# A second LayerNorm whose half sums are put together on GpSimd, a piece at a time

## The chip, the core and the metric

The kernel runs on one core of a Trainium2 chip. The metric is device time in microseconds of one launch. The engines that matter here are VectorE (DVE in the profile), GpSimd (POOL), ScalarE (ACT), TensorE (PE) and SyncE (SP, which issues DMAs). Each engine takes the instructions of its own queue strictly in order, and engines wait for one another through semaphores.

## What is computed

The reference is one layer in two halves on `x` of shape (4, 1024, 256). The first half is a Mamba block (gated selective scan) with a residual and a LayerNorm; the second is a mixture of experts (one shared expert and the best two of eight) with a residual and a second LayerNorm:

```
def _layernorm(x, axis=-1, eps=1e-05):
    m = jnp.mean(x, axis=axis, keepdims=True)
    v = jnp.var(x, axis=axis, keepdims=True)
    return (x - m) / jnp.sqrt(v + eps)
...
    x = _layernorm(x + _L0_attn_ref(x, ...), axis=-1)
    x = _layernorm(x + _L0_ffn_ref(x, ...), axis=-1)
    return x
```

The change is in the second of these two LayerNorms: for each of 4096 tokens, the mean and variance of 256 numbers, and then (x - m) / sqrt(v + 1e-5).

## The kernel before

**The long part.** The 4096 tokens are cut into 8 chunks of 512 (`CHUNKS`). For each chunk and each of 16 states the loop over `order` runs a scan (`scan`, `outputs`). Beside it, generators are advanced a step at a time: `front` (projections and convolution of the next chunk), `tail` (output projection, first LayerNorm, router and the lists of rows by expert of the chunk before) and `moe` (the experts' matrix products, block by block). Experts' results are added by DMA into a buffer in device memory, `sums_of`, which already holds the first LayerNorm's output.

**The end.** After all experts there is a conditional block for blocks left over (no instruction crosses it), and then `finish()` (L1003 on). It is the only caller of the second LayerNorm. It cuts the 32 tiles of 128 tokens into five pieces of 4, 8, 8, 8 and 4 tiles, and issues at once, on SyncE, the five loads of the pieces from `sums_of` into SBUF tiles `o_0` to `o_4` (L1011). Then, for each piece in turn:

1. `stats` (L215 to L220, called in the loop over `pieces`, L1038): for each tile of 128 tokens a VectorE `bn_stats` (L219) writes six numbers a token: count, mean, and sum of squared deviations, for each of two halves of the row; a VectorE `bn_aggr` (L220) puts the halves together into mean and variance, `mv`.
2. A VectorE instruction adds 1e-5 to the variances of the piece (`var`, L1043).
3. `rsqrt` (L204 to L212): a first guess by integer arithmetic, and three Newton steps of four instructions each, 13 instructions in all, each of which needs the one before. Its tiles are [128, tiles of the piece]. It runs on GpSimd for the first four pieces and on VectorE for the last (`newton`).
4. On the same engine, `shift` = -(mean x rstd), two instructions (L1047, L1048).
5. `scale` of the piece **before** this one: 5 of 8 tiles (3 of 4) on ScalarE (L1023), the rest on VectorE (L1029), and two stores, one on ScalarE's queue (L1034) and one on SyncE's (L1035). The last piece is scaled after the loop.

The buffers of `small` are double: `mv2`, `var2`, `root`, `nt` and `shift` each have two, so piece i+2 takes the buffer of piece i, and can write it only when its last reader is done. The last readers of `root` and `shift` are the `scale` instructions.

**Order.** The framework lays out each engine's queue before the run, with the program's order as priority, but an instruction that it holds to be ready may be put ahead of one that it holds to be waiting. The order is then fixed, and so are the waits. Only what is marked `keep_in_program_order` (the VectorE part of `scale`) is bound.

The lines outside `finish` that the diff touches are in `tail` and `by_expert`, once a chunk: `probs` (L626, router), `row` (L688), `mine` (L652 and L692) and `ee` (L749).

Of the kernel before, what the change touches and what calls it, by code (L numbers as in the profile page):

```python
# [8 lines left out]
F32 = mybir.dt.float32  # L9
AF = mybir.ActivationFunctionType  # L10
ALU = mybir.AluOpType
AX = mybir.AxisListType

P = 128
NSEQ, SEQ, D = 4, 1024, 256
# [5 lines left out]
E = 8  # L21
# [49 lines left out]
def mamba_moe_kernel(  # L71
# [18 lines left out]
    nc = tc.nc  # L90

    const = ctx.enter_context(tc.tile_pool(name="const", bufs=1))
    small = ctx.enter_context(tc.tile_pool(name="small", bufs=2))
    one = ctx.enter_context(tc.tile_pool(name="one", bufs=1))
# [105 lines left out]
    def rsqrt(v, name, engine=nc.gpsimd):  # L200

        shape = list(v.shape)
        y = small.tile(shape, F32, tag="root", name=f"root_{name}")
        engine.tensor_scalar(  # L204
            y.bitcast(I32), v.bitcast(I32), -0.5, float(0x5F3759DF), ALU.mult, ALU.add
        )
        t = small.tile(shape, F32, tag="nt", name=f"nt_{name}")
        for _ in range(3):
            engine.tensor_tensor(t, y, y, ALU.mult)  # L209
            engine.tensor_tensor(t, t, v, ALU.mult)  # L210
            engine.tensor_scalar(t, t, -0.5, 1.5, ALU.mult, ALU.add)  # L211
            engine.tensor_tensor(y, y, t, ALU.mult)  # L212
        return y

    def stats(src, mv, tiles, name):  # L215

        for t in range(tiles.start, tiles.stop):
            st = small.tile([P, 6], F32, tag="bnst", name=f"bnst_{name}_{t}")
            nc.vector.bn_stats(st, src[:, t, :])  # L219
            nc.vector.bn_aggr(mv[:, t, :], st)  # L220
# [320 lines left out]
    def tail(b, c):  # L541
        s = f"{b}_{c}"
# [13 lines left out]
        mv = small.tile([P, TT, 2], F32, tag="mv", name=f"mv_{s}")  # L556
        for half in range(2):
            po = ps_mix.tile([P, TT // 2, D], F32, tag="mix", name=f"po_{s}_{half}")
            for i in range(TT // 2):
                t = half * TT // 2 + i  # L560
# [17 lines left out]
        var = small.tile([P, 2, TT], F32, tag="var", name=f"var_{s}")  # L578
# [3 lines left out]
        rstd = rsqrt(var, f"l1_{s}")  # L582
# [18 lines left out]
        few = [P, TT, E]  # L601
# [21 lines left out]
        scaled(summed, rstd[:, 0, :], mv[:, :, 0], summed, f"l1_{s}")  # L623
        nc.scalar.dma_start(own_sums.rearrange("(t p) d -> p t d", p=P), summed)
        yield
        probs = small.tile(few, F32, tag="probs", name=f"probs_{s}")  # L626
        nc.scalar.activation(probs, logits, AF.Sigmoid)
        nc.scalar.activation(probs2, logits, AF.Sigmoid)
        full = [P, TT, E, E]
# [1 line left out]
        own = probs.unsqueeze(3).to_broadcast(full)  # L631
# [20 lines left out]
        mine = one.tile([P, TOPK, TT, E], F32, tag="mine", name=f"mine_w_{s}")  # L652
# [19 lines left out]
        nc.scalar.copy(combT, pc)  # L672
        channels[b, c] = (x1T, combT)
        yield from by_expert(b, c, hn, rank, weights, both, sofar, part, flat)

    def by_expert(b, c, hn, rank, weights, both, sofar, part, flat):

        s = f"{b}_{c}"
# [3 lines left out]
        few = [P, TT, E]  # L682
# [2 lines left out]
        nc.tensor.matmul(place[:, 0:TT, :], lhsT=upper, rhs=both, start=False, stop=True)  # L685
        yield from wait(1, 2)
        counts = place[:, TT, :]
        row = one.tile(few, F32, tag="row", name=f"row_{s}")  # L688
        nc.vector.tensor_tensor(
            row, place[:, 0:TT, :], starts.unsqueeze(1).to_broadcast(few), ALU.add  # L690
        )
        mine = one.tile([P, TOPK, TT, E], F32, tag="mine", name=f"mine_{s}")  # L692
# [53 lines left out]
        nc.vector.tensor_reduce(so_far, over, AX.X, ALU.add)  # L746
        nc.vector.tensor_tensor(there, so_far, done, ALU.subtract)
        nc.vector.tensor_tensor(left, so_far, done, ALU.subtract)
        ee = one.tile([P, E, E], F32, tag="ee", name=f"ee_{s}")  # L749
        nc.vector.tensor_tensor(ee, before, left.unsqueeze(1).to_broadcast([P, E, E]), ALU.mult)  # L750
        scatter(0)
        yield from wait(1, 2)
# [250 lines left out]
    def finish():  # L1003


        tags = ["xs", "delta", "y"]
        pieces, at = [], 0
        for i, tiles in enumerate((4, 8, 8, 8, 4)):
            o = two.tile([P, tiles, D], F32, tag=tags[i % 3], name=f"o_{i}")
            rows = slice(at * P, (at + tiles) * P)  # L1010
            nc.sync.dma_start(  # L1011
                o, sums_of[P + rows.start : P + rows.stop, :].rearrange("(t p) d -> p t d", p=P)
            )
            dst = out.rearrange("b s d -> (b s) d")[rows, :].rearrange("(t p) d -> p t d", p=P)
            pieces.append((o, dst))
            at += tiles

        def scale(o, dst, rstd, shift):
            tiles = o.shape[1]
            on_act = (5 * tiles + 4) // 8  # L1020
            for t in range(tiles):
                if t < on_act:
                    nc.scalar.activation(  # L1023
                        o[:, t, :], o[:, t, :], AF.Identity,
                        bias=shift[:, t : t + 1], scale=rstd[:, t : t + 1],
                    )
                else:
                    tc.keep_in_program_order(
                        nc.vector.tensor_scalar(  # L1029
                            o[:, t, :], o[:, t, :], rstd[:, t : t + 1], shift[:, t : t + 1],  # L1030
                            ALU.mult, ALU.add,
                        )
                    )
            nc.scalar.dma_start(dst[:, 0:on_act, :], o[:, 0:on_act, :])  # L1034
            nc.sync.dma_start(dst[:, on_act:, :], o[:, on_act:, :])  # L1035

        ahead = None
        for i, (o, dst) in enumerate(pieces):  # L1038
            tiles = o.shape[1]
            mv = small.tile([P, tiles, 2], F32, tag="mv2", name=f"mv2_{i}")  # L1040
            stats(o, mv, slice(0, tiles), f"l2_{i}")
            var = small.tile([P, tiles], F32, tag="var2", name=f"var2_{i}")
            nc.vector.tensor_scalar(var, mv[:, :, 1], 1e-5, None, ALU.add)  # L1043
            newton = nc.gpsimd if i + 1 < len(pieces) else nc.vector
            rstd = rsqrt(var, f"l2_{i}", newton)
            shift = small.tile([P, tiles], F32, tag="shift", name=f"shift_l2_{i}")
            newton.tensor_tensor(shift, mv[:, :, 0], rstd, ALU.mult)  # L1047
            newton.tensor_scalar(shift, shift, -1.0, 0.0, ALU.mult, ALU.add)  # L1048
            if ahead is not None:
                scale(*ahead)  # L1050
            ahead = o, dst, rstd, shift
        scale(*ahead)


# [33 lines left out]
    for i, step in enumerate(order):  # L1088
# [3 lines left out]
        for k in range(KB):  # L1092
# [15 lines left out]
            if k == KB // 2 - 1:  # L1108
                if late is not None:
                    outputs(*late)  # L1110
                    if n == 0:
                        list_of = ending if place + 1 == len(chunks) else beside
                        list_of.append(tail(*chunks[place - 1]))
                if n == 0 and place + 1 < len(chunks):
                    beside.append(front(*chunks[place + 1]))
                if n == 3:
                    beside.append(scans[b, c][4]())
                if n == N // 2 and place + 2 < len(chunks):
                    xs_in[chunks[place + 2]] = load_x(*chunks[place + 2])
                side(beside)  # L1120
# [9 lines left out]
    keep(*late[0:2])  # L1130
    outputs(*late)
    ending.append(tail(*chunks[-1]))
    while ending:
        side(ending)
# [5 lines left out]
    with tc.If(left > 0):  # L1140
        first, last = last, last + len(at_end)
        units += at_end
        for u in range(first, last):
# [5 lines left out]
            while pending:  # L1149
                pending.pop(0)()  # L1150
    finish()


# [52 lines left out]
```

## Time and profile before

| what | value |
|---|---|
| time, median of 3 runs (lowest, highest) | 1592.58 us (1586.84, 1595.74) |
| the profiled execution, its own time | 1591.91 us |
| its span, first to last instruction | 1590.2 us |
| loads of the five pieces issued (L1011) | from 1556.16 us |
| first `bn_stats` of piece 0; of piece 1 | 1560.00 us; 1563.29 us |
| ScalarE starts scaling pieces 0, 1, 2, 3 | 1566.30, 1571.64, 1576.20, 1580.81 us |
| last store issued | 1584.96 us |
| `bn_stats` (L219), `bn_aggr` (L220) in the end stage | 32 of 410 ns, 32 of 178 ns (median) |
| small GpSimd instructions of the stage | 60, about 200 ns each |

All times of instructions are counted from the start of the span. The stage in question is its last 34 us, 2% of it. A line of the timeline has the start, the time from the start of its first to the end of its last instruction, the engine, the line of the code, the operation, out<-in with shapes, the number of instructions, and in brackets how long the engine had been idle and who released it. Consecutive instructions of one engine can overlap in these records: a start may lie before the end of the one before.

### The profile page before, as it was taken

The page shows a single profiled execution, that of the slowest core. Times are in us where ns is not written, and L with a number is a line of the kernel's source. Part 1 is how long each engine was busy: PE and PEld are TensorE (multiplying, and loading weights), DVE is VectorE, ACT ScalarE, POOL GpSimd, SP SyncE. Part 2 cuts the span into 40 slices and gives each one's busy share as a digit, 9 for nine tenths or more (in the row PEclk, how much of TensorE's full clock was granted, in tenths as well). Part 3 has the DMA queues.
Part 4 walks back from the last instruction along what each step waited for, and adds up shares of the span by engine and source line. Part 5 has one row for each costly group of instructions (what it writes and reads, how often), then busy time and mean ns, then how long its engine had stood idle before and what let it go on. Part 6 is the DMA issues. An engine that isn't in the chain of part 4 may idle for free. (4 is left out here: it accounts for less than half of the span.)

```text
span 1590.2 us, 20804 instructions
## 1 busy us (share of the span) xinstructions
PE 1254.7 (79%) x6639; PEld 970.3 (61%) x6639; DVE 1279.8 (80%) x1422; ACT 1065.6 (67%) x2345; POOL 1141.6 (72%) x886
## 2 busy tenths in 40 slices
PE   5588467865688788879798889888879889899990
PEld 2356324652356666677567756776667768789990
DVE  3999899989997898999998999899989899320005
ACT  5757458764778578877788778766886666434442
POOL 2468975798578876998789978997699887431223
PEclk8699678987788999999999999899899999999995
DMA  4000000440016562475236633563166538659996
GB/s 121 1 0 1 26 14 17 146 119 17 13 61 192 173 182 64 147 220 168 50 124 204 190 80 122 159 197 107 35 209 185 153 116 249 177 153 323 315 273 217
DMA packets 160275, 211.64 MB, mean 133 GB/s; under 512 B 20617, under 2 KB 138130, under 8 KB 160162
## 3 DMA queue, kind: packets, MB, share of 16 engines
q1 hardware_dynamic: 135954, 181.75, 35.2%
q0 software_dynamic: 17216, 21.57, 7.6%
q10 hardware_dynamic: 6992, 6.95, 1.3%
q8 instruction: 54, 0.88, 0.2%
q14 instruction: 59, 0.48, 0.1%
HBM read 178.97 MB, written 31.27 MB: 132 GB/s over the span
## 5 line engine op out<-in xcount | busy, mean ns | idle before, releaser
L530 POOL TENSOR_TENSOR y<-y,hs 128x2048 f32<-128x2048 f32 x128 | 597.1, 4665 | 81.2 <-DVE hs L529 80.8
L513 ACT ACTIVATE da<-delta,chan_sb 128x512 f32<-128x512 f32 x512 | 353.0, 697 | 193.1 <-DVE hs L516 190.6
L929 PE MATMUL pd<-w,h 128*128 128x256 f32 x1600 | 386.7, 386 | 22.5 <-ACT h L909 11.5
L929 PEld LDWEIGHTS pd<-w,h 128*128 128x128 f32 x1600 | 298.8, 193 | 92.8 <-issue 20.5
L516 DVE TENSOR_TENSOR_SCAN hs<-da,state,hs 128x512 f32<-128x512 f32 x256 | 317.8, 1270 | 27.1 <-ACT da L513 26.0
L900 PEld LDWEIGHTS pu<-xT,w 128*128 128x128 f32 x2176 | 276.6, 204 | 64.7 <-ACT xT L883 45.5
L900 PE MATMUL pu<-xT,w 128*128 128x128 f32 x2176 | 281.3, 288 | 28.0 <-ACT xT L883 28.0
L529 DVE TENSOR_TENSOR hs<-hs,pb 128x2048 f32<-128x2048 f32 x128 | 290.7, 2271 | 3.3 <-PE pb L430 1.6
L909 ACT ACTIVATE h<-pu,wb 128x128 f32<-128x128 f32 x800 | 229.3, 368 | 71.9 <-PE pu L900 67.2
L516 DVE TENSOR_TENSOR_SCAN hs<-da,hs 128x512 f32<-128x512 f32 x204 | 240.9, 1209 | 21.2 <-ACT da L513 20.7
L449 POOL TENSOR_TENSOR hs<-xs,b 128x512 f32<-128x512 f32 x118 | 170.6, 1448 | 67.9 <-ACT b L442 48.9
L444 DVE TENSOR_TENSOR hs<-xs,pb 128x1536 f32<-128x1536 f32 (+1 forms) x115 | 197.9, 1722 | 13.2 <-ACT b L442 7.5
L962 POOL DMA_INDIRECT sums<-rb,xb x68 | 108.0, 1588 | 131.3 <-ACT xT L883 43.8
L293 PE MATMUL pi<-hT,w_in_sb 128*128 128x512 f32 x256 | 143.0, 683 | 32.6 <-DVE xs L325 12.3
L430 PE MATMUL pb<-parts,pick 128*128 128x512 bf16 x243 | 98.2, 407 | 77.1 <-DVE hs L529 27.6
L900 PEld LDWEIGHTS pu<-x1T,w 128*128 128x128 f32 x1024 | 130.9, 203 | 13.8 <-issue 10.0
L900 PE MATMUL pu<-x1T,w 128*128 128x128 f32 x1024 | 136.4, 290 | 0.0
L219 DVE BATCH_NORM_STATS2 bnst_l<-o 128x6 f32<-128x256 f32 x32 | 11.9, 411 | 153.9 <-DMA o<-sums 153.9
L293 PEld LDWEIGHTS pi<-hT,w_in_sb 128*128 128x128 f32 x256 | 49.9, 213 | 97.3 <-issue 34.2
L562 PE MATMUL po<-w_out_sb,y 128*128 128x256 f32 x256 | 70.0, 435 | 36.6 <-POOL y L552 29.1
L562 PEld LDWEIGHTS po<-w_out_sb,y 128*128 128x128 f32 x256 | 55.5, 222 | 56.3 <-POOL y L552 36.3
L705 POOL DMA_INDIRECT rows<-hn,to x64 | 63.4, 990 | 32.1 <-issue 15.8
(198 smaller groups left out, 1555.8 us busy)
## 6 DMA issues: line engine op xcount, KB each, us to landing
w<-in_ew SPq DMA_DIRECT2D x136, 1024.0 KB, 5.7
w<-in_sw SPq DMA_DIRECT2D x16, 1024.0 KB, 5.3
xb<-rows SPq DMA_DIRECT2D x68, 129.0 KB, 5.1
x<-in_x SPq DMA_DIRECT2D x8, 512.0 KB, 4.2
sums<-summed ACTq DMA_DIRECT2D x8, 512.0 KB, 3.0
sums<-rs POOLq DMA_DIRECT2D x16, 256.0 KB, 6.6
o<-sums SPq DMA_DIRECT2D x3, 1024.0 KB, 8.8
out<-o ACTq DMA_DIRECT2D x3, 640.0 KB, 3.3
```

The costliest lines, as they stand in the source:

```text
L293: nc.tensor.matmul(pi, lhsT=w_in_sb[:, k, m * P : (m + 1) * P], rhs=hT[:, k, :], start=(k == 0), stop=(k == KD - 1),)
L444: nc.vector.tensor_tensor(hs[:, 0:on_pool, :], xs[:, 0:on_pool, :], pb.unsqueeze(1).to_broadcast([P, on_pool, TC]), ALU.mult,)
L449: nc.gpsimd.tensor_tensor(hs[:, k, :], xs[:, k, :], copy, ALU.mult)
L513: nc.scalar.activation(da, delta[:, k, :], AF.Exp, scale=chan_sb[:, k, CA + n : CA + n + 1])
L516: nc.vector.tensor_tensor_scan(hs[:, k, :], da, scaled_inputs.pop(0) if by_pe(step) else hs[:, k, :], 0.0 if c == 0 else state[:, k, n : n ...
L529: nc.vector.tensor_tensor(hs, hs, pb.unsqueeze(1).to_broadcast([P, KB, LEN[b, c]]), ALU.mult)
L530: nc.gpsimd.tensor_tensor(y, y, hs, ALU.add)
L562: ins = nc.tensor.matmul(po[:, i, :], lhsT=y[:, k, t * P : (t + 1) * P], rhs=w_out_sb[:, k, :], start=(k == 0), stop=(k == KB - 1),)
L900: nc.tensor.matmul(pu[:, i, :], lhsT=w[:, k, at : at + P], rhs=xT[:, k, :], start=(k == 0), stop=(k == KD - 1),)
L909: nc.scalar.activation(t[:, i, :], pu[:, i, :], AF.Relu, bias=wb[:, m : m + 1])
L929: nc.tensor.matmul(pd, lhsT=hidden[h][:, i, :], rhs=w[:, m, :], start=(m == 0), stop=(m == HB - 1 and e is None),)
L962: nc.gpsimd.indirect_dma_start(sums_of[:, :], bass.IndirectOffsetOnAxis(xb[:, TOKEN : TOKEN + 1].bitcast(U32), 0), rb, None, compute_op=AL ...
```

## The change

The loop over the pieces calls one of two functions. The last piece takes `own`: what was done before, all on VectorE. The first four take `by_halves`: VectorE runs only the `bn_stats`, into one tile `halves` of [128, tiles, 6]; the `bn_aggr` of each tile and the VectorE instruction for `var` are gone. GpSimd then makes variance and mean of all the tiles of the piece with strided operands: six instructions for `var` (difference of the two means, its square, a quarter of it plus 1e-5; sum of the two sums of squares, divided by 256; the sum of both), the same `rsqrt`, and three for `shift` (sum of the means, times `rstd`, times -0.5) where there were two. That is 22 GpSimd instructions a piece in place of 15. To make room in SBUF, three small tiles of the long part share buffers: `probs` has one buffer in place of two, `row` lies in the tag `o` (used otherwise in the set-up only), and `ee` in the tag `mine`.

```diff
-        probs = small.tile(few, F32, tag="probs", name=f"probs_{s}")
+        probs = small.tile(few, F32, tag="probs", name=f"probs_{s}", bufs=1)
...
-        row = one.tile(few, F32, tag="row", name=f"row_{s}")
+        row = one.tile(few, F32, tag="o", name=f"row_{s}")
...
-        ee = one.tile([P, E, E], F32, tag="ee", name=f"ee_{s}")
+        ee = one.tile([P, E, E], F32, tag="mine", name=f"ee_{s}")
...
+        def own(i, o):
+            tiles = o.shape[1]
+            mv = small.tile([P, tiles, 2], F32, tag="mv2", name=f"mv2_{i}")
+            stats(o, mv, slice(0, tiles), f"l2_{i}")
+            var = small.tile([P, tiles], F32, tag="var2", name=f"var2_{i}")
+            nc.vector.tensor_scalar(var, mv[:, :, 1], 1e-5, None, ALU.add)
+            rstd = rsqrt(var, f"l2_{i}", nc.vector)
+            shift = small.tile([P, tiles], F32, tag="shift", name=f"shift_l2_{i}")
+            nc.vector.tensor_tensor(shift, mv[:, :, 0], rstd, ALU.mult)
+            nc.vector.tensor_scalar(shift, shift, -1.0, 0.0, ALU.mult, ALU.add)
+            return rstd, shift
+
+        def by_halves(i, o):
+            tiles = o.shape[1]
+            st = small.tile([P, tiles, 6], F32, tag="halves", name=f"halves_{i}")
+            for t in range(tiles):
+                nc.vector.bn_stats(st[:, t, :], o[:, t, :])
+            var = small.tile([P, tiles], F32, tag="var2", name=f"var2_{i}")
+            apart = small.tile([P, tiles], F32, tag="nt", name=f"apart_{i}")
+            shift = small.tile([P, tiles], F32, tag="shift", name=f"shift_l2_{i}")
+            g = nc.gpsimd
+            g.tensor_tensor(apart, st[:, :, 1], st[:, :, 4], ALU.subtract)
+            g.tensor_tensor(apart, apart, apart, ALU.mult)
+            g.tensor_scalar(apart, apart, 0.25, 1e-5, ALU.mult, ALU.add)
+            g.tensor_tensor(var, st[:, :, 2], st[:, :, 5], ALU.add)
+            g.tensor_scalar(var, var, 1.0 / D, 0.0, ALU.mult, ALU.add)
+            g.tensor_tensor(var, var, apart, ALU.add)
+            rstd = rsqrt(var, f"l2_{i}", g)
+            g.tensor_tensor(shift, st[:, :, 1], st[:, :, 4], ALU.add)
+            g.tensor_tensor(shift, shift, rstd, ALU.mult)
+            g.tensor_scalar(shift, shift, -0.5, 0.0, ALU.mult, ALU.add)
+            return rstd, shift
+
         def scale(o, dst, rstd, shift):
...
         for i, (o, dst) in enumerate(pieces):
             tiles = o.shape[1]
-            mv = small.tile([P, tiles, 2], F32, tag="mv2", name=f"mv2_{i}")
-            stats(o, mv, slice(0, tiles), f"l2_{i}")
-            var = small.tile([P, tiles], F32, tag="var2", name=f"var2_{i}")
-            nc.vector.tensor_scalar(var, mv[:, :, 1], 1e-5, None, ALU.add)
-            newton = nc.gpsimd if i + 1 < len(pieces) else nc.vector
-            rstd = rsqrt(var, f"l2_{i}", newton)
-            shift = small.tile([P, tiles], F32, tag="shift", name=f"shift_l2_{i}")
-            newton.tensor_tensor(shift, mv[:, :, 0], rstd, ALU.mult)
-            newton.tensor_scalar(shift, shift, -1.0, 0.0, ALU.mult, ALU.add)
+            rstd, shift = (own if i + 1 == len(pieces) else by_halves)(i, o)
             if ahead is not None:
                 scale(*ahead)
```

## The prediction

> **What bounds the kernel now.** I first read the page's rows by slices of the span, to see where the change lies.
>
> ```profile
> span 1590.2 us, 20804 instructions
> DVE  3999899989997898999998999899989899320005
> ACT  5757458764778578877788778766886666434442
> POOL 2468975798578876998789978997699887431223
> ```
>
> A slice is 39.8 us. All that the change computes differently lies in the last one, where no engine is busy by more than half: a stage of latencies, with all else finished. Its length adds to the kernel one to one. So I read next who waits for whom from 1556 us on, where the loads of the second LayerNorm are issued.
>
> ```profile
> engine line waited for: us in total, times, longest us
> DVE bnst_l L219 <- DMA o<-sums: 153.9, 2, 152.7
> ACT o L1023 <- POOL shift_l L1048: 18.9, 3, 14.9
> POOL root_l L204 <- DVE var L1043: 10.0, 4, 8.5
> ```
>
> ScalarE waits for GpSimd's `shift`, GpSimd for VectorE's `var`, VectorE for the loads: a relay. Which runner is slow is seen in the order of time, VectorE around the end of piece 1:
>
> ```profile
> 1566.56 0.30 DVE L220 BATCH_NORM_AGGREGATE mv<-bnst_l 128x2 f32<-128x6 f32 x2
> 1566.78 0.41 DVE L219 BATCH_NORM_STATS2 bnst_l<-o 128x6 f32<-128x256 f32 x1
> 1567.11 0.15 DVE L1043 TENSOR_SCALAR var<-mv 128x8 f32<-128x8 f32 x1
> 1567.17 0.41 DVE L1029 TENSOR_SCALAR o<-o,root_l,shift_l 128x256 f32<-128x256 f32 x1
> 1567.49 0.17 DVE L220 BATCH_NORM_AGGREGATE mv<-bnst_l 128x2 f32<-128x6 f32 x1
> ```
>
> and GpSimd at the same place:
>
> ```profile
> 1565.79 0.20 POOL L1047 TENSOR_TENSOR shift_l<-mv,root_l 128x4 f32<-128x4 f32 x1
> 1566.08 0.19 POOL L1048 TENSOR_SCALAR shift_l<-shift_l 128x4 f32<-128x4 f32 x1
> 1567.34 0.29 POOL L204 TENSOR_SCALAR root_l<-var 128x8 int32<-128x8 int32 x1 [1.07 <-DVE var L1043]
> 1567.72 0.20 POOL L209 TENSOR_TENSOR nt_l<-root_l 128x8 f32<-128x8 f32 x1
> ```
>
> Two things are to be seen. GpSimd works on one piece at a time, each instruction 0.28 us after the one that it needs (1565.79 to 1566.08), though it is busy for only 0.20; it finished piece 0 at 1566.27 and had to wait for the `var` of piece 1. Its four chains end at 1566.27, 1571.61, 1576.17 and 1580.78: one each 4.6 us, of which about 4.3 is the chain and the rest the wait for VectorE. And the order isn't the program's: at 1566.78 VectorE does the first `bn_stats` of piece 2 **ahead** of the `var` of piece 1, for whose input it would have had to wait. An instruction that is held to be ready fills such a gap. Does that happen on GpSimd too? In the first LayerNorm it does:
>
> ```profile
> 1383.71 0.20 POOL L212 TENSOR_TENSOR root_l<-root_l,nt_l 128x8 f32<-128x8 f32 x1
> 1383.99 0.20 POOL L239 TENSOR_TENSOR shift_n<-mv,root_l 128x4 f32<-128x4 f32 x1
> 1384.14 0.20 POOL L239 TENSOR_TENSOR shift_l<-mv,root_l 128x4 f32<-128x4 f32 x1
> 1384.30 0.20 POOL L240 TENSOR_SCALAR shift_n<-shift_n 128x4 f32<-128x4 f32 x1
> 1384.46 0.20 POOL L240 TENSOR_SCALAR shift_l<-shift_l 128x4 f32<-128x4 f32 x1
> ```
>
> Two independent pairs are interleaved, though the second is written much later, and then an instruction starts 0.155 us after the one before, not 0.28. Two chains side by side cost 0.31 a pair of steps, hardly more than one chain alone. This pair of numbers decides the case.
>
> The stage ends with ScalarE, whose own work follows GpSimd's last `shift`:
>
> ```profile
> 1580.81 3.06 ACT L1023 ACTIVATE o<-o,shift_l,root_l 128x256 f32<-128x256 f32 x6 [2.04 <-POOL shift_l L1048]
> 1583.40 0.39 ACTq L1034 DMA_DIRECT2D out<-o  x1
> 1583.84 1.09 ACT L1023 ACTIVATE o<-o,shift_l,root_l 128x256 f32<-128x256 f32 x2
> ```
>
> From 1580.81 it is 9.4 us to the end of the span (eight tiles, two stores, landing), and nothing in the change touches these. So the forecast is: when is `shift` of piece 3 done?
>
> **What is removed.** 28 `bn_aggr` and four `var` on VectorE. Two `bn_stats` and two `bn_aggr` take 0.88 us (1563.29 to 1564.17), 0.44 a tile; a `bn_stats` alone follows another after 0.33 (a pair lasts 0.75, the second 0.41). So 0.11 us a tile, 3.1 us of VectorE in all, and 0.1 to 0.2 for each `var`. A piece of 8 is ready after 7 x 0.33 + 0.41 = 2.7 us in place of 3.9. The bound from above is that a lone `bn_stats` keeps its whole 0.41: then 3.3 and only 1.6 us saved; I take 0.33, which the trace shows whenever two are neighbours. Also gone is a 0.37 us wait at 1571.36, where `bn_aggr` of piece 3 waited for the buffer of `mv`.
>
> **What is added.** Seven GpSimd instructions a piece, 28 in all. Nearest row for each: the 0.20 us instructions on 128x8. Their operands now have a stride of 24 bytes; the nearest strided row is L337, 211 ns for 4 elements and 355 for 8 in two dimensions, so 0 to 0.15 us for each of three such instructions; I take 0, since theirs is one dimension. As a chain, four of the seven come in front of `root` (difference, square, scale, sum); the other two of `var` and the sum of the means need nothing of these and can fill gaps. `shift` itself has two left behind `rstd`, as now. The chain is then 19 instructions, 18 x 0.284 + 0.20 = 5.3 us, with the fillers 5.4, against 14 x 0.284 + 0.20 = 4.2 now.
>
> Here a rule speaks against the change: the Trainium skill, "GPSIMD Engine Reference", section "Engine selection", sends elementwise work to VectorE, with GpSimd about twice as slow on two inputs. VectorE's own chain on the last piece steps at 0.2 us (1579.01, 1579.22, 1579.41). By the rule the seven cost 7 x 0.4 = 2.8 us a piece, 11.2 in all; put end to end with four chains of 4.3 from 1561.5, GpSimd would end at 1589.9, 9 us later than now. By the rows they cost 0.155 to 0.284 each, 1.1 to 2.0 a piece. On 8 elements the factor of two isn't there (0.20 busy against 0.16 to 0.17), so I go by the rows.
>
> **The sum.** Piece 0: four `bn_stats` from 1560.00 end at 1561.40, GpSimd starts 0.1 later (as now after `var`), ends 1566.9 (now 1566.27). Piece 1: loaded at 1563.29, `bn_stats` end at 1566.0, start 1566.1; 5.4 plus 0.03 for each of some 11 steps that it shares with pieces 0 and 2: 1571.8 (now 1571.61). Piece 2: its load lands near 1566.3 (1 MB at the 0.35 MB/us of the DMA row in these slices); `bn_stats` and one scaled tile to 1569.3; chain to 1575.2 (now 1576.17), side by side with the end of piece 1. Piece 3: landed near 1569.6, `bn_stats` to 1572.3, first four steps to 1573.6; but its `root` and `shift` take the buffers of piece 1, which ScalarE reads until 1571.85 + 2.56 = 1574.4. This is the new wait: behind it stand on GpSimd only steps of piece 2 that come late in its chain. From 1574.5, 15 instructions, 4.2 us and 0.1 of sharing: 1578.8, now 1580.78. ScalarE ends piece 2 at 1577.8, so it is free. The last piece on VectorE (`root` from 1577.8, for the buffer of piece 2, then 15 x 0.2) is ready at 1580.9, before ScalarE comes to it at 1581.4. Gain: 2.0 us. If `nt` of piece 3 must wait as well for that of piece 2, it is 1.3. Had GpSimd only one chain at a time, the same 1.1 us a piece would be lost instead: the cover is the gap-filling.
>
> **Edits outside the stage** cost nothing by the profile: `row`, `mine` and `ee` are written and read by VectorE alone, in order, and `ee` is written 1.3 us after the last reader of `mine`. `probs` has its last reader within 3 us and is written again a chunk later, over 100 us. If the framework lays out the long part otherwise because of them, the cost can have either sign; no row sizes it, and I leave up to 10 us for it.
>
> The profiled execution has 1591.91 us, 1.7 over its span; minus 2.0 gives 1589.9. The median of the runs is 0.67 higher: 1590.6.
>
> **Rivals.**
> *One chain at a time (slower).* GpSimd keeps the written order and each piece has 22 instructions: 19 steps at 0.284 and three independent ones at 0.155 make 5.9 us, against some 3 in which VectorE now delivers a piece. GpSimd then never waits, and its queue is the bound: 1561.5 + 4 x 5.9 + 0.6 for collisions with VectorE's scaling (0.24 to 0.32 us at 1571.80) = 1585.6 to 1587.1, if all steps take 0.284. That is 4.8 to 6.3 later, 1598 at the middle. It decides as soon as pieces aren't interleaved, for 22 steps don't fit into the 4.6 us of a piece. For it: GpSimd shows no interleaving in this stage now. Against: it had never two pieces ready now.
> *The order misjudges the loads.* Steps of the next piece are placed into a chain earlier than their data come, and the chain stands still behind them. Data of piece 1 are known to come late: between its chain's start and 1566.1 at most 1.5 us can be lost on piece 0, which has slack, and as much on piece 1 or 2, which has none: 0.5 less to 3 more than before, 1594 at the middle.
> *The change does nothing that shows:* the tags move the long part, either sign, 1582 to 1602.
>
> **How the numbers follow.** Interleaved, 3 to 0.5 us gained: 0.58. Order misjudged: 0.16. One chain at a time: 0.17. Long part moved: 0.09. The three runs lie 9 us apart, so a median is good to some 3 us; 0.5% (8 us, about what a measurement of this kernel can tell from no change) is more than any case but the last gives alone. Faster by more: 0.09 (the first case with luck, half of the last). Slower by more: 0.14 (a third of the serial case, some of the second, half of the last). The range goes from the first case less 4.6, 1586.0, to the serial one, 1598.5.
>
> **What would show it.** Right: VectorE's `bn_stats` 0.33 us apart; on GpSimd, steps of two pieces alternating at 0.155; its last `shift` near 1578.8, 18.8 us after the first `bn_stats`, now 20.8; ScalarE ending piece 1 just before `root` of piece 3. Wrong: GpSimd busy without a gap from 1561.5 to 1586 with one piece after the other; waits of GpSimd for `bn_stats` in mid-chain; or a first `bn_stats` far from 1560.

## The result and the profile after

The changed kernel is slower: 1593.93 us against 1590.07 (medians of 23 runs each), ratio 1.0031 with a 95% interval of 1.0018 to 1.0044, that is 3 to 7 us. The forecast was a gain of 2 us. The loss is within the 0.5% that was called "no change", but clear of zero, and it has the other sign.

The profiled execution happens to be the longest of the 23 (1604.44 us), so its span says little. Up to `finish` every engine has the same instructions in the same order in both kernels, and 9.4 us of this execution's excess lie there: its first `bn_stats` of the last stage starts at 1569.43, before it was 1560.00. The edits outside the stage don't explain it: experiments 1 to 6 below have the same three, and there the first `bn_stats` start at 1555.44 to 1560.32. From here on the stage is measured from that first `bn_stats`, which takes this difference out.

| from the first `bn_stats` of piece 0, us | before | after |
|---|---|---|
| last `shift` of GpSimd done | 20.78 | 24.89 |
| last store issued by ScalarE | 24.96 | 29.07 |
| end of the span | 30.20 | 33.27 |

So the stage lost 4.1 us to the last store and 3.1 to the end. (From the last store's issue to the end it takes 5.2 us before and 4.2 after. The DMA engines moved 340 GB/s there before, from 1584.0 to 1588.5, and 385 after, from 1595.5 to 1601.0; why, no run shows.) The DMA engines are not what slowed the stage: up to the last `shift` they are less busy than before, a share of 0.62 against 0.84. Where does the loss come from? First the waits of the changed kernel from the stage's beginning on (who waited for whom, sum, number, longest):

```profile
DVE halves L1037 <- DMA o<-sums: 161.1, 2, 159.6
ACT o L1059 <- POOL shift_l L1051: 31.5, 4, 20.4
POOL apart L1042 <- DVE halves L1037: 7.7, 1, 7.7
DVE o L1065 <- POOL shift_l L1051: 6.5, 3, 2.6
```

GpSimd waited for VectorE four times before; now once, at the start, and never again. VectorE, which waited for GpSimd once before, by 0.4 us, now does so three times, 6.5 us in all. The runner that sets the pace has changed. In order of time, VectorE's row of the same kernel:

```profile
1572.32 2.71 DVE L1037 BATCH_NORM_STATS2 halves<-o 128x6 f32<-128x256 f32 x8 [1.48 <-DMA o<-sums]
1576.57 0.45 DVE L1065 TENSOR_SCALAR o<-o,root_l,shift_l 128x256 f32<-128x256 f32 x1 [1.54 <-POOL shift_l L1051]
1576.93 2.70 DVE L1037 BATCH_NORM_STATS2 halves<-o 128x6 f32<-128x256 f32 x8
1582.27 1.09 DVE L1065 TENSOR_SCALAR o<-o,root_l,shift_l 128x256 f32<-128x256 f32 x3 [2.64 <-POOL shift_l L1051]
```

The statistics of a piece of 8 take 2.7 us, as forecast, in place of 3.7 to 4.0 (before, from 1563.29 and from 1572.62 to the end of `var`), and the gain ends in the brackets: 1.54 and 2.64 us of waiting. And GpSimd, at the end of piece 0 and the start of piece 1:

```profile
1575.77 0.20 POOL L212 TENSOR_TENSOR root_l<-root_l,nt_l 128x4 f32<-128x4 f32 x1
1576.05 0.20 POOL L1050 TENSOR_TENSOR shift_l<-shift_l,root_l 128x4 f32<-128x4 f32 x1
1576.34 0.19 POOL L1051 TENSOR_SCALAR shift_l<-shift_l 128x4 f32<-128x4 f32 x1
1576.49 0.21 POOL L1042 TENSOR_TENSOR apart<-halves 128x8 f32<-128x8 f32 x1
1576.66 0.21 POOL L1045 TENSOR_TENSOR var<-halves 128x8 f32<-128x8 f32 x1
1576.82 0.26 POOL L1049 TENSOR_TENSOR shift_l<-halves 128x8 f32<-128x8 f32 x1
```

The first three lines are 0.28 us apart, each waiting for the one before; the last three, which need nothing of one another, follow at 0.16 to 0.17. So gaps are filled within a piece (the sum of the means, L1049, is written as the last but two of 22 and comes third). But the statistics of piece 1 were done at 1575.03, and no step of piece 1 stands in the gaps of piece 0 after that. GpSimd does one piece after the other: pieces begin at 1570.92, 1576.49, 1582.19 and 1588.20, and the last ends at 1594.32.

The loss can be added up. The four chains took 17.1 us before and take 23.4 now, 6.3 more. GpSimd starts 0.65 us earlier than before, and the waits between chains, 1.6 us in all, are gone. What is left is 4.1 us.

At the end of the stage ScalarE's row has the same eight tiles, now behind a `shift` that is later:

```profile
1588.28 2.56 ACT L1059 ACTIVATE o<-o,shift_l,root_l 128x256 f32<-128x256 f32 x5 [3.44 <-POOL shift_l L1051]
1594.36 0.60 ACT L1059 ACTIVATE o<-o,shift_l,root_l 128x256 f32<-128x256 f32 x1 [3.52 <-POOL shift_l L1051]
1594.36 0.38 ACTq L1070 DMA_DIRECT2D out<-o  x1
```

There is an oddity: the store of piece 2, whose tiles were done at 1590.84, stands behind the first tile of piece 3 and so goes out at 1594.36. It looks as if the layout had held piece 3 to be ready by then.

### The profile page after: what moved, and what is told of

Read it like the earlier page. It is cut to its first block, busy times and chain, and to the rows that moved or that the text cites. A ratio compares the mean times of both kernels' runs of the same rounds, so it can differ in the third digit from the quotient of the medians.

```text
span 1602.7 us, 20797 instructions
## 1 busy us (share of the span) xinstructions
PE 1261.7 (79%) x6639; PEld 971.3 (61%) x6639; DVE 1276.2 (80%) x1390; ACT 1066.5 (67%) x2345; POOL 1146.4 (72%) x914
## 5 line engine op out<-in xcount | busy, mean ns | idle before, releaser
L929 PE MATMUL pd<-w,h 128*128 128x256 f32 x1600 | 387.6, 387 | 23.4 <-ACT h L909 11.3
L1037 DVE BATCH_NORM_STATS2 halves<-o 128x6 f32<-128x256 f32 x28 | 9.5, 408 | 161.1 <-DMA o<-sums 161.1
```

What stands on the lines that cost most here:

```text
L929: nc.tensor.matmul(pd, lhsT=hidden[h][:, i, :], rhs=w[:, m, :], start=(m == 0), stop=(m == HB - 1 and e is None),)
```

## The experiments

**Theory S**, formed on this profile: GpSimd's queue, one chain of 22 instructions after another, sets the end; what VectorE saves is lost in waiting. Rivals: the shared tags moved the long part (T); VectorE's saving still counts (V); the buffers kept the pieces from being interleaved (B). Each kernel has one profile, but the stage repeats well: with the stage as before the last `shift` comes at 20.78 and 20.75 us, with the changed one at 24.89, 24.88 and 24.73 (experiments 1, 2 and 5).

**1. Only the tags** (the three lines for `probs`, `row` and `ee`, with `finish` as before).

> The second LayerNorm as before; only the three tags in the long part are shared (probs, row, ee). Theory S (serial chains: the end of the kernel is set by GpSimd doing one piece after another, 22 steps each): no difference to before, within 2 us, and the last shift of GpSimd 20.8 us after the first bn_stats, as before. Rival T (the shared tags moved the long part): most of the 4 to 5 us that the changed kernel loses is here, with the last stage as before.

Ratio to before 1.0004 (0.9988 to 1.0020), last `shift` at 20.75 us. T falls: the stage is as before, and the long part shows no cost of the tags. The interval alone leaves room for 2 us less to 3 us more; that the stage starts no later in the profiles of experiments 1 to 6, which all have these edits, speaks against a cost as well.

**2. The saving undone**

```diff
                 nc.vector.bn_stats(st[:, t, :], o[:, t, :])
+                nc.vector.bn_aggr(unused[:, t, :], st[:, t, :])
```

> The changed kernel, with the bn_aggr of each tile put back on VectorE; nothing reads what they write. Theory S: VectorE has some 2 us of slack a piece behind GpSimd, so 0.11 us a tile costs at most the 0.4 us of the first piece: last shift 24.9 to 25.4 us after the first bn_stats, the time of the changed kernel within 2 us. Rival V (VectorE's saving still counts at the end, and hides a larger loss on GpSimd): 2 to 3 us slower than the changed kernel.

Last `shift` at 24.88 us, against 24.89 without them. The 28 `bn_aggr` are free here: with GpSimd's chains as they are, what the change takes off VectorE is worth nothing. (Ratio 1.0015, 0.9997 to 1.0033, which overlaps that of the changed kernel.) V falls.

**3. Four instructions fewer a piece** (the changed kernel, with a coarser root)

```diff
-            rstd = rsqrt(var, f"l2_{i}", g)
+            rstd = rsqrt(var, f"l2_{i}", g, 2)
```

> The changed kernel with two Newton steps in place of three on GpSimd in the second LayerNorm (a coarser inverse root for four of the five pieces): 18 instructions a piece in place of 22. Theory S: each GpSimd instruction of the stage lies on the path; 4 x 4 x 0.284 = 4.5 us less than the changed kernel, so about the time of before; last shift 20.4 us after the first bn_stats. Rival T: nothing but noise, for the stage isn't what was lost.

Last `shift` at 20.21 us, 4.7 less than the changed kernel for 16 instructions: 0.29 us each, the full step. Ratio 0.9987 (0.9970 to 1.0004), the interval lying wholly below that of the changed kernel. These 16 instructions are on the path with all of their time, as S says of every step of the chain.

**4. The order written out**

```diff
+        steps_of(15, c[0])
+        steps_of(7, c[0], c[1])
...
+        steps_of(11, c[1], c[2])
...
+        steps_of(11, c[2], c[3])
...
+        steps_of(11, c[3])
```

> The changed kernel with the same 22 GpSimd instructions a piece, but their order written out: a piece starts when the one before is about two thirds through, and from there their steps alternate (buffers for all pieces, so no slot waits). Theory S with the prediction's row of 0.155 us: pairs of steps 0.31 us apart, last shift 19.3 us after the first bn_stats, 5 us less than the changed kernel and 1 to 2 less than before. Rival P (alternating steps don't overlap on GpSimd while VectorE and ScalarE work; each costs 0.28): as the changed kernel, 24.9 us.

GpSimd's row in that kernel, where piece 2 (L1048, L1049) begins beside the Newton steps of piece 1 (L1059, L1060):

```profile
1567.35 0.21 POOL L1048 TENSOR_TENSOR scratch<-scratch 128x8 f32<-128x8 f32 x1
1567.51 0.20 POOL L1059 TENSOR_TENSOR scratch<-scratch 128x8 f32<-128x8 f32 x1
1567.67 0.20 POOL L1049 TENSOR_TENSOR scratch<-scratch 128x8 f32<-128x8 f32 x1
1567.83 0.20 POOL L1060 TENSOR_TENSOR scratch<-scratch 128x8 f32<-128x8 f32 x1
```

Two chains do run at 0.32 us a pair here; the row that the prediction rested on holds in this stretch. Last `shift` at 21.60 us, 3.3 less than the changed kernel, ratio 0.9995 (0.9978 to 1.0012). But I had expected 19.3. Three things are seen in the row: piece 0 stood for 0.6 us behind the first step of piece 1, put there before its statistics were done; ten gaps in the alternation were still 0.28 in place of 0.16 (as at L1053, 1569.09 and 1573.63), 1.2 us in all, for which I have no cause; and two steps at 1571.57 and 1571.89, beside VectorE's scaling, lasted 0.35 to 0.37, 0.3 us. By this estimate they make up most of the 2.3 us. The written order differs on VectorE too: the statistics run one piece further ahead of the scaling (piece 2 from 1563.73, piece 0 scaled at 1566.36), so that GpSimd has two pieces to work on. So the order of the two engines together was the difference between loss and no loss, but even this order gives no gain over before.

**5. Were it the buffers?** The chain of experiment 4 with its own room for every piece, written piece after piece, and the order left to the framework.

> The 22 GpSimd instructions a piece of the changed kernel, with buffers for every piece of their own (no tile of the chain is shared between pieces), written piece after piece and left to the framework's order. Theory O (the framework holds a chain to be over before the next statistics are there, so it sees nothing to fill with): still one chain after another, last shift 24.9 us after the first bn_stats, as the changed kernel. Rival B (the double buffers of halves, nt, root and shift kept the next piece out): with buffers free, the pieces alternate, and the last shift comes near 21.6 us, as in the interleaved kernel.

Still one chain after another: pieces begin at 1558.34, 1563.88, 1569.55 and 1575.51, last `shift` at 24.73. The statistics of piece 2 are done at 1567.02, and GpSimd runs piece 1 to its end at 1569.59 before it takes them up:

```profile
1564.32 2.70 DVE L1039 BATCH_NORM_STATS2 scratch<-o 128x6 f32<-128x256 f32 x8
1569.39 0.20 POOL L1064 TENSOR_SCALAR scratch<-scratch 128x8 f32<-128x8 f32 x1
1569.55 0.21 POOL L1048 TENSOR_TENSOR scratch<-scratch 128x8 f32<-128x8 f32 x1
```

B falls. (Ratio 1.0010, 0.9992 to 1.0028.)

**6. The half sums on VectorE**

```diff
-            g = nc.gpsimd
+            g = nc.vector
```

> The changed kernel with the half sums put together by seven VectorE instructions a piece on 128x8 in place of seven on GpSimd; GpSimd has the inverse root and two instructions of shift, 15 as before. Theory S (what counts is the length of GpSimd's queue): GpSimd is back to a chain of 4.3 us a piece; VectorE needs 2.7 + 7 x 0.2 + 1.1 = 5.2 us a piece and is now the slower, so last shift 21 to 22.5 us after the first bn_stats, 2.5 to 4 less than the changed kernel, within 2 us of before. Rival: merging by halves costs the same wherever it is done, 24.9 us.

Last `shift` at 22.26 us; ratio 1.0005 (0.9992 to 1.0018). The size is as S has it, GpSimd's chains are short again (4.2 us from `root` to `shift`), but they start 5.3 us apart, at 1564.73, 1570.03 and 1575.30, each after a wait of 1.0 to 1.1 us for `var`. My reason for that was not right: the seven VectorE instructions are cheap, 0.09 us each where they are independent. VectorE's row shows what happened instead:

```profile
1568.99 0.41 DVE L1065 TENSOR_SCALAR o<-o,root_l,shift_l 128x256 f32<-128x256 f32 x1 [1.50 <-POOL shift_l L1051]
1569.32 0.17 DVE L1044 TENSOR_SCALAR apart<-apart 128x8 f32<-128x8 f32 x1
...
1569.71 0.16 DVE L1047 TENSOR_TENSOR var<-var,apart 128x8 f32<-128x8 f32 x1
```

The last two steps to `var` of piece 2 stand behind the scaling of piece 1, which waits for GpSimd; GpSimd then waits for `var`. Each engine is idle while the other works.

**7. No chain at all** (kernel before, all on VectorE and ScalarE)

```diff
-            var = small.tile([P, tiles], F32, tag="var2", name=f"var2_{i}")
-            nc.vector.tensor_scalar(var, mv[:, :, 1], 1e-5, None, ALU.add)
-            newton = nc.gpsimd if i + 1 < len(pieces) else nc.vector
-            rstd = rsqrt(var, f"l2_{i}", newton)
+            rstd = small.tile([P, tiles], F32, tag="root", name=f"root_l2_{i}")
+            nc.scalar.activation(rstd, mv[:, :, 1], AF.Sqrt, bias=eps)
+            nc.vector.reciprocal(rstd, rstd)
+            newton = nc.vector
```

> The kernel before, with the 13 instructions of the inverse root replaced by a square root on ScalarE and a reciprocal on VectorE, shift on VectorE, bn_aggr kept; the framework's order, scaling one piece behind as before. Theory S says that the chain of dependent small GpSimd instructions is what the stage is made of: without it VectorE is the bound, 3.5 + 0.6 + 1.1 = 5.2 us a piece from 3.3 us on; last store issued near 23 us after the first bn_stats, where before has 25.0. Rival: the stage is bound by ScalarE's scaling and the stores, then 25 as before.

Last store issued at 22.28 us, where before has 24.96; ratio 0.9986 (0.9969 to 1.0003). The last store comes 2.7 us earlier, so the chain of small GpSimd instructions was a bound of the stage before as well. The time itself isn't clear of no change.

**8. The change's idea with a short chain**: half sums on GpSimd, square root on ScalarE, reciprocal and one instruction of `shift` on VectorE, their order written out.

```diff
+        ahead = None
+        for i, (o, dst) in enumerate(pieces):
...
+            halves(st, o, range(early))
+            if ahead is not None:
+                root(*ahead[2:])
+            halves(st, o, range(early, tiles))
+            if ahead is not None:
+                scale(*ahead)
+            ahead = o, dst, *together(i, st)
```

> GpSimd puts the half sums together (the seven instructions of the change, all five pieces), ScalarE takes the square root, VectorE the reciprocal and the shift, and the order on VectorE and ScalarE is written out, so that a piece is scaled while the statistics of the next one are made. Theory S: with no long chain on GpSimd the removed bn_aggr count at last: a piece each 3.1 us (the pace of the loads), last store issued 19 to 20.5 us after the first bn_stats against 25.0 before and 29.1 in the changed kernel; 4 to 6 us less than before, ratio 0.997. Rival: the half sums on GpSimd cost what they save anywhere, about 25.

Ratio 0.9967 (0.9952 to 0.9982): 3 to 8 us faster than before, and the only kernel here whose interval lies clear of before on the faster side. Last store at 22.08 us, end of the span at 25.79 (before: 30.20). It is less than I expected at the last store: a piece takes 3.3 to 4.0 us and not the 3.1 of the loads. ScalarE's row near the end, and VectorE's for the piece before and for this one:

```profile
1574.87 2.56 ACT L1050 ACTIVATE o<-o,shift_l,root_l 128x256 f32<-128x256 f32 x5 [0.73 <-DVE shift_l L1043]
1577.46 0.38 ACTq L1061 DMA_DIRECT2D out<-o  x1
1577.89 0.21 ACT L1038 ACTIVATE root_l<-var 128x8 f32<-128x8 f32 x1 [0.46 <-ACT o L1050]
1578.64 2.56 ACT L1050 ACTIVATE o<-o,shift_l,root_l 128x256 f32<-128x256 f32 x5 [0.54 <-DVE shift_l L1043]
...
1572.40 2.06 DVE L1022 BATCH_NORM_STATS2 halves<-o 128x6 f32<-128x256 f32 x6
1574.37 0.19 DVE L1042 RECIPROCAL root_l<-root_l 128x8 f32<-128x8 f32 x1
1578.13 0.20 DVE L1042 RECIPROCAL root_l<-root_l 128x8 f32<-128x8 f32 x1 [0.69 <-ACT root_l L1038]
```

From 1574.87 to 1578.64 ScalarE has hardly room: scaling, the issue of the store, the root, and a short wait for VectorE's reciprocal. For the last two pieces this loop through ScalarE is the bound. For the pieces before it is VectorE, which has next to no idle time from 1565.15 to 1577.44: at 1574.37 its reciprocal stands behind six `bn_stats`, though ScalarE's root was done at 1574.14. The next limit may be the DMA engines, which no run here varies: the stage moves 8.4 MB (4.2 in and as much out), which at the 350 GB/s of its busiest stretch (1564 to 1572) is 24 us by estimate, and from the first load's issue (1557.89) to the end it now takes 29.8.

**9. Which part of 8 was it?** The same order and square root, with `bn_aggr` on VectorE in place of the half sums, so that GpSimd is idle.

> The kernel with the square root on ScalarE and the written order, but with bn_aggr on VectorE in place of the half sums on GpSimd: GpSimd does nothing in the stage. It differs from the version with half sums on GpSimd in that one thing. If the 0.11 us a tile of bn_aggr count once the chain is short, VectorE needs 0.9 us more for each of three pieces, less the 1.5 us that GpSimd's seven instructions take at the end of the last piece: last store issued 22.5 to 24.5 us after the first bn_stats (the version with half sums: 22.1; before: 25.0), 0 to 2 us slower than that version and still 1 to 3 us faster than before. If moving the half sums is worth nothing or a loss even here, 21 to 22 us.

Last store at 24.30 us, 2.2 later than in experiment 8, end of the span at 28.34; ratio to before 0.9991 (0.9970 to 1.0012). So in this order moving the half sums to GpSimd is worth some 2 us of the stage, once GpSimd isn't the bound; the two intervals of the time overlap. The square root alone in this fixed order gains 0.7 us at the last store and 1.9 at the end. In the framework's order (experiment 7) its last store is at 22.28, but the span ends at 27.75; why it needs 5.5 us for that, and 4.0 here, no run shows.

## Why the prediction was wrong, point by point

- **Right:** what bounds the stage (a relay in which ScalarE waits for GpSimd); VectorE's 0.33 us a `bn_stats` (2.71 for eight); next to no extra cost of strided operands (0.21 us against 0.20; the third of them, L1049, lasts 0.26 beside VectorE's scaling); 0.155 us between independent GpSimd instructions (mostly 0.155 to 0.17); edits outside the stage at nothing (experiment 1; the last reader of `probs` comes up to 8.4 us after it, not within 3, which changes nothing). A chain of 5.4 us was a little short: it took 5.6 to 6.1, the longer ones beside VectorE's scaling, where some GpSimd steps last 0.35 instead of 0.20.
- **The step that failed:** "Had GpSimd only one chain at a time, the same 1.1 us a piece would be lost instead: the cover is the gap-filling." The cover wasn't there. I had seen gaps filled where both instructions were ready at that point, and took it that a piece would be filled in beside another. The queue is laid out before the run, and the profile after shows it laid out piece after piece, with buffers free or not (experiment 5). I gave this case 0.17, as a rival, with 4.8 to 6.3 us; it came, with 4.1 at the last `shift`. It came as the prediction's own sign of being wrong had it, with GpSimd busy without a gap and one piece after the other. Its sum was a little dear: the four pieces took 5.6, 5.7, 6.0 and 6.1 us, 23.4 in all, where it had 24.2 and more.
- **What hid in the evidence:** that "GpSimd shows no interleaving in this stage now" I answered with "it had never two pieces ready". That is true in the record, but it says nothing of what the layout takes to be ready. Why the layout puts the next piece behind the whole chain isn't shown by any run. The store of piece 2 that stands behind the first tile of piece 3 fits a layout that takes GpSimd's chain for much shorter than it is; this is argued, not shown.
- **A second term that was mis-sized:** even with the pieces interleaved, my sum (18.8 us to the last `shift`) was too good. By hand it came to 21.6. The gain of 2 us wasn't there in the order that I tried.
- **The rule and the row:** by the rule of the Trainium skill ("GPSIMD Engine Reference", section "Engine selection") that GpSimd is about twice as slow on two inputs, the prediction had GpSimd end at 29.9 us after the first `bn_stats`. That sum doubled all seven instructions; only five of them have two inputs, which makes it 28.3, an estimate from the same figures. It ended at 24.9: on 128x8 the rows were the better guide for the size, and the rule had the sign right.

## What to carry to other kernels

In a relay of engines, ask for each piece how long each engine's own part is, one after another as its queue stands: before, VectorE and GpSimd were nearly even (about 4.6 and 4.3 us a piece), so making GpSimd's part 1.6 us longer lost 1.0 us a piece (the rest came out of waits that it had before), and shortening VectorE's by about 1 gained nothing (experiment 2). Count on overlap within one engine's queue only if the profile shows it between those very pieces, or if you write the order out. And look at the longest chain of dependent small instructions first: replacing 13 of them by two on other engines brought the end of the stage from 30.2 to 27.8 us, where no placement of the half sums with the chain kept came below 30.2. With the chain gone the change's own idea gained too, by 2.2 us at the last store, and gave the only time that is clearly better than before (experiments 8 and 9).

## What was not expected of the hardware

- Small VectorE instructions that need nothing of one another start 0.08 us apart while each lasts 0.16 (experiment 6: 1558.71, 1558.79, 1558.87); dependent ones are 0.20 apart. On GpSimd the same two numbers are 0.155 and 0.284. One instruction doesn't fit: L1044 of the changed kernel comes 0.28 after L1046 (1577.21, 1577.49), of which it needs nothing; no run shows why.
- GpSimd steps of 0.20 us last up to 0.35 while VectorE scales tiles with operands per partition (at 1582.75 and 1583.07, beside L1065 from 1582.27 to 1583.36; one at 1582.36 still took 0.21). They keep 0.20 beside VectorE's `bn_stats` and ScalarE's scaling together (1583.78 to 1584.63). That VectorE's scaling is the cause is argued from this coincidence, not tested.
